# A two-layer graph attention network: the first layer's edge weights and running sums in a PSUM bank, the node chain in one bank instead of two

## The chip, the core and the metric

The kernel runs on one core of one Trainium2 chip. The metric is device time in microseconds of one launch. Most executions of one kernel agree within 0.3%. Five engines matter here: PE (matrix products), DVE (vector work), ACT (activations and copies), POOL (here it issues the indirect DMAs) and SP (here it issues the plain DMAs). PSUM is the small memory that PE writes its products to; it has eight banks of 512 float32 values in each of 128 partitions. SBUF is the large on-chip memory.

## What is computed

A graph of 6250 nodes (16 node types) and 100000 edges (32 edge types), sorted by destination, goes through two layers of typed attention and a residual normalisation. With the names of the reference, cut to what matters:

```
def gt_layer(x, ntype, etype, src, dst, Wk, Wq, Wv, Wa, Watt, Wmsg, pri, skip, g, b):
    k = typed_linear(x, ntype, Wk).reshape(n, H, HS)
    q = typed_linear(x, ntype, Wq).reshape(n, H, HS)
    v = typed_linear(x, ntype, Wv).reshape(n, H, HS)
    kT = jnp.einsum('nhd,htdo->nhto', k, Watt)
    vT = jnp.einsum('nhd,htdo->nhto', v, Wmsg)
    kw = kT[src, :, etype]
    m = vT[src, :, etype]
    a = jnp.einsum('ehd,ehd->eh', kw, q[dst]) * pri[:, etype].T / SQRT_D
    att = edge_softmax(a, dst, n)
    msg = (m * att[:, :, None]).reshape(-1, H * HS)
    hag = jax.ops.segment_sum(msg, dst, num_segments=n)
    h = jax.nn.silu(typed_linear(hag, ntype, Wa))
    alpha = jax.nn.sigmoid(skip[ntype])[:, None]
    h = h * alpha + x * (1.0 - alpha)
    mu = jnp.mean(h, axis=-1, keepdims=True)
    var = jnp.mean((h - mu) ** 2, axis=-1, keepdims=True)
    return (h - mu) * jax.lax.rsqrt(var + 1e-05) * g + b

for l in range(L):
    h = gt_layer(h, ...)
return layernorm(x + h @ ff_w + ff_b)
```

`typed_linear` takes a matrix for each node type; kT and vT hold a row for each node and edge type; L = 2. There are H = 8 heads of HS = 16, so a row of k, q or v has 128 values.

## The kernel before

**Stages.** A first stage sorts the nodes into 49 blocks of 128 (one node to a partition) by type and by number of edges, and builds the first layer's table in DRAM: for each node and edge type one row of 256 values, kT and vT side by side. Then `edges(0)` runs the first layer and, beside it, builds the second layer's table; `edges(1)` runs the second layer and writes the output.

**Gathers.** For a block with K slots (K is the largest number of edges of its nodes), POOL issues K indirect DMAs (L1434). Each brings one table row to each of the 128 partitions. There are 819 in each layer. Behind each stand two small fills of a tile called `pause` (L1440), also on POOL. Four gathers fill one tile `kv` (a chunk, CH = 4); twelve such tiles are in turn, so POOL waits when the oldest is not yet used up.

**A block's edge work, on DVE.** For each chunk: `kv*q` (L1454) and a sum over each head (L1460) give the logits `a`. Then `finished` (L1298 to L1375) does for the block: add the mask, subtract the largest, `Exp` on ACT (L1323), and for each chunk the product of the values with the weights (L1339) and the addition to `acc` (L1346). `acc` has four slots of 128 values, so that a chunk is added in one instruction; at the end a reduction over the four slots gives `sums` (L1367). In the first layer the weights stand in `a` and the sums in `acc`, both in SBUF. In the second layer the query, the weights and the sums stand in a PSUM tile `pair` of the pool `tps` (L1285, L1322, L1334). One block, `TOP`, with 42 slots, has a way of its own in both layers.

**The node chain.** Two to four blocks make a superblock, 15 in all. Thirteen hold nodes of four types; two hold blocks of all 16 types and are called mixed here (`len(types) > TC`). When a superblock's sums are there, the generator `nodes` (L1536) turns the sums (transposes on PE into a tile `hT`), multiplies a copy of `hT` masked by type (`xm`, on DVE, L271) with `wa` for each type, applies the gate, the skip and the normalisation, and turns the result again. In the first layer it then makes k, v and q for the next layer (`wkqv`): k and v are copied from PSUM to SBUF (`kvT0`, `kvT1`, by ACT), q is turned back and stored. From `kvT` PE makes the pieces of the second layer's table (`tb<-bdk,kvT`, L312), ACT copies them to `st` (L320), and POOL scatters each `st` to DRAM (L1672, 98 scatters in all, two for each block). The queries of the first layer, `queries0` (L1219), go through the same steps with `wq0`. All these tiles that are written by PE have the name `nb` and come from the pool `nps`, two banks of PSUM. The pool `tps` has three tiles of two banks. That fills the eight banks.

**The order of the work.** POOL's instructions run in the order of the program. The generators of the node chain and of the queries are advanced by a few steps for each chunk of gathers: `tick` (L1249) spreads a given number of steps (33 for a node chain of the first layer, 42 more when mixed) over the slots of the blocks that follow. A scatter is issued eight such steps after its last piece. On PE, DVE and ACT a scheduler then sets the order; instructions that go through `on` appear in the trace under the line of a helper, L247. The second layer's gathers wait for all 98 scatters.

## Time and profile before

| | us |
|---|---|
| three timed runs | 3146.17, 3147.55, 3155.6 (median 3147.55) |
| the profiled execution's own time | 3152.49 |
| its span, from the first to the last instruction | 3150.6 |
| POOL busy | 2376.3 (75%) |
| DVE busy | 1871.8 (59%) |
| PE busy | 1561.5 (50%) |
| ACT busy | 964.4 (31%) |

The first layer's gathers start at 594 us and its last one at 1887 us of the span; the second layer's start at 1958 us and end at 3105 us. A row that groups instructions reads: line, engine, operation, output and inputs by the program's names, shape, count, then the busy time in us and the mean of one in ns, and behind the bar the time for which the engine was idle just before them, with what ended it. In a row of the timeline the two numbers in front are the start and the duration in us, and in brackets stands how long the engine had been idle before, with what ended that. PE's records hold two passes for each float32 product, so four products are eight records.

### The profile page before, as it was taken

Reading aid. Unit: us, or ns where it says so; the run is one execution under the profiler, and the core shown is the slowest. Engines: PE = TensorE matmul, PEld = TensorE weight load, DVE = VectorE, ACT = ScalarE, POOL = GpSimd, SP = SyncE. Lnnn points to the kernel's source line nnn. Section 1 sums busy time; section 2 is a strip of 40 time slices with the busy share of each in tenths; the row PEclk is TensorE's granted clock in tenths of the full one; section 3 lists DMA queues with packets and bytes.
Section 4 is the critical chain, followed back from the end, with each engine's and each line's share of the span. In section 5 each row is a group of like instructions: output and inputs, shape, how many; then the busy total and the mean of one; then the engine's idle time right before and its main releaser. Section 6 shows DMA issues by size and latency. Waiting matters only on the chain.

```text
span 3150.6 us, 24725 instructions
## 1 busy us (share of the span) xinstructions
PE 1561.5 (50%) x5295; PEld 706.2 (22%) x5295; DVE 1871.8 (59%) x4322; ACT 964.4 (31%) x1599; POOL 2376.3 (75%) x5392
## 2 busy tenths in 40 slices
PE   5999887303675647776688775011221122112112
PEld 2445334101232312332233232000110011001001
DVE  7477655266646656666665553466556675666565
ACT  3887433101444123533354453001100121012111
POOL 3332665588868887888888882888788888888884
PEclk9899766556677767777777686555555556555555
DMA  7999999933777457775688888333333333333331
GB/s 214 421 419 414 390 388 399 299 94 101 256 262 274 157 194 262 279 295 195 233 306 297 304 290 313 104 109 107 99 102 103 110 114 106 100 108 108 98 97 46
DMA packets 174584, 674.80 MB, mean 214 GB/s; under 512 B 52972, under 2 KB 89998, under 8 KB 149374
## 3 DMA queue, kind: packets, MB, share of 16 engines
q0 software_dynamic: 113152, 635.19, 56.1%
q1 hardware_dynamic: 45170, 30.78, 3.4%
q10 hardware_dynamic: 16096, 7.10, 0.9%
q8 instruction: 46, 0.75, 0.1%
q14 instruction: 120, 0.98, 0.1%
HBM read 248.64 MB, written 425.02 MB: 214 GB/s over the span
## 4 chain that ended last, share of the span: by engine, by line
POOL 46%; issue 11%; DMA 10%; DVE 8%; PE 5%; ACT 2%; POOLq 0%; DVEq 0%; ACTq 0%
POOL kv L1434 35%; DMA kv<-tab,ell 9%; POOL pause L1440 7%; PE nb L247 3%; POOL tab L1672 1%; DMA tab<-st,row 1%; DVE kv L1454 1%; POOL out_dram L1704 1%; PE tb L312 1%; DVE kv L247 1%; DVE hs L247 1%; DVE a L1460 1%; DVE acc L247 1%; ACT L247 1%; ACT st L320 1%
## 5 line engine op out<-in xcount | busy, mean ns | idle before, releaser
L1434 POOL DMA_INDIRECT kv<-tab,ell x1638 | 1634.1, 998 | 325.6 <-issue 250.0
L320 ACT COPY st<-tb 128x512 f32<-128x512 f32 (+1 forms) x984 | 677.5, 778 | 555.6 <-PE tb L312 330.4
L1454 DVE TENSOR_TENSOR kv<-kv,tb 128x512 f32<-128x512 f32 (+3 forms) x223 | 143.0, 641 | 449.0 <-DMA kv<-tab,ell 443.6
L1454 DVE TENSOR_TENSOR kv<-kv,q 128x512 f32<-128x512 f32 (+3 forms) x223 | 143.6, 645 | 410.5 <-DMA kv<-tab,ell 404.1
L247 PE MATMUL nb<-ident,hag 128*128 128x128 f32 x98 | 27.1, 417 | 722.2 <-DVE hag L247 722.1
L1440 POOL MEMSET pause<- 128x32 bf16 x3276 | 334.2, 142 | 0.7
L312 PE MATMUL tb<-bdv,kvT 32*128 32x512 f32 x784 | 259.4, 799 | 52.3 <-ACT st L320 51.7
L312 PE MATMUL tb<-bdv,vT 32*128 32x512 f32 x784 | 260.2, 784 | 48.8 <-ACT st L320 45.0
L1460 DVE TENSOR_REDUCE a<-kv 128x32 f32<-128x512 f32 (+2 forms) x446 | 281.5, 634 | 1.2
L1128 POOL DMA_INDIRECT tab<-st,rows x98 | 101.6, 1037 | 199.5 <-ACT st L320 165.3
L247 PE MATMUL nb<-xm,wa 128*128 128x512 f32 (+2 forms) x336 | 187.3, 715 | 106.0 <-DVE xm L247 105.8
L312 PE MATMUL tb<-bdk,kvT 32*128 32x512 f32 x784 | 231.9, 776 | 14.1 <-ACT st L320 13.7
L247 PE MATMUL nb<-xm,wkqv 128*128 128x384 f32 (+2 forms) x504 | 209.5, 579 | 20.8 <-DVE xm L247 20.8
L318 DVE COPY st<-tb 128x512 f32<-128x512 f32 (+1 forms) x192 | 128.7, 708 | 147.6 <-PE tb L312 78.3
L312 PE MATMUL tb<-bdk,kT 32*128 32x512 f32 x784 | 206.0, 783 | 6.5 <-issue 5.8
L247 PEld LDWEIGHTS nb<-ident,hag 128*128 128x128 f32 x98 | 16.1, 205 | 740.5 <-issue 510.5
L247 DVE SCALAR_TENSOR_TENSOR xm<-ntb,nb 128x512 f32<-128x512 bf16 (+2 forms) x304 | 155.3, 562 | 40.0 <-PE nb L247 39.8
L247 PE MATMUL nb<-xm,wq 128*128 128x384 f32 (+2 forms) x168 | 88.5, 678 | 163.4 <-DVE xm L247 163.4
L1672 POOL DMA_INDIRECT tab<-st,row x98 | 104.1, 1062 | 83.7 <-ACT st L320 59.9
L247 PEld LDWEIGHTS nb<-xm,wkqv 128*128 128x128 f32 x504 | 111.7, 228 | 126.0 <-issue 45.5
L247 DVE TENSOR_TENSOR tb<-kv,tb 128x512 f32<-128x512 f32 (+3 forms) x216 | 138.6, 642 | 0.2
L247 PE MATMUL nb<-ident,hs 128*128 128x128 f32 x98 | 33.5, 469 | 205.6 <-DVE hs L247 198.4
(342 smaller groups left out, 2467.8 us busy)
## 6 DMA issues: line engine op xcount, KB each, us to landing
kv<-tab,ell POOLq DMA_INDIRECT x1638
hr<-xrd SPq DMA_DIRECT2D x14, 256.0 KB
hqd<-hs SPq DMA_DIRECT2D x7, 512.0 KB, 3.1
hq<-hqd SPq DMA_DIRECT2D x7, 512.0 KB
xrd<-xr SPq DMA_DIRECT2D x10, 256.0 KB, 23.2
hr<-xrd SPq DMA_DIRECT2D x10, 192.0 KB, 2.8
hqd<-hs SPq DMA_DIRECT2D x5, 384.0 KB
hq<-hqd SPq DMA_DIRECT2D x5, 384.0 KB, 3.2
```

What stands on the lines that cost most here:

```text
L247: put = issue(*args, **kwargs)
L312: stream[nc.tensor] = nc.tensor.matmul(pt[:, b], yT[s, i * P:(i + 1) * P], bd[s, tt, :], start=True, stop=True)
L318: nc.vector.tensor_copy(to, pt)
L320: stream[nc.scalar] = nc.scalar.copy(to, pt)
L1128: put = nc.gpsimd.indirect_dma_start(out=tabs[0].rearrange("(n t) c -> n (t c)", t=16), out_offset=bass.IndirectOffsetOnAxis(ap=rows1[:, t ...
L1434: get = nc.gpsimd.indirect_dma_start(out=kv[:, j - j0, :], out_offset=None, in_=tabs[l][:], in_offset=bass.IndirectOffsetOnAxis(ap=ell[:, ...
L1440: nc.gpsimd.memset(pause[:, at % PAUSES, half], 0.0)
L1454: stream[nc.vector] = nc.vector.tensor_tensor(kk, kk, of.unsqueeze(1).to_broadcast([P, c, D]), op=ALU.mult)
L1460: nc.vector.tensor_reduce(to, kk.rearrange("p k (h d) -> p k h d", h=H), axis=AX.X, op=ALU.add)
L1672: put = nc.gpsimd.indirect_dma_start(out=tabs[1].rearrange("(n t) c -> n (t c)", t=16), out_offset=bass.IndirectOffsetOnAxis(ap=row2[:, tg ...
L1704: put = nc.gpsimd.indirect_dma_start(out=out, out_offset=bass.IndirectOffsetOnAxis(ap=node[:, b:b + 1], axis=0), in_=o[:, i, :], in_offset ...
```

## The change

Three things change together. All are in the arm that the run takes (`fast`).

1. The first layer's weights and running sums go to a PSUM tile `held` of one bank (pool `hold`, one buffer): two slots of sums of 128 values each, and the weights behind them. `Exp` writes the weights there, and the products and additions read and write there. Since the sums are two slots wide and not four, a chunk of four is added in two instructions; the first chunk's first two slots go to the sums as products, and its other two are added afterwards. The block `TOP` keeps its way.
2. For that bank, the pool `nps` of the node chain and the queries has one bank instead of two. A new function `linear_of` takes the output's tile only when the masked copies of `hT` have been made; where a superblock is mixed, `hT` is first copied to SBUF (`h2`), in both layers.
3. A mixed superblock makes k, v and q one after the other, each with masked copies of its own, and no longer k and v from the same copies. The table of steps gives a mixed node chain of the first layer 58 steps more and not 42.

```
+    def linear_of(pool, nps, types, ntb, hT, n, w):
+        types = list(types)
+        if len(types) > TC:
+            h2 = pool.tile([P, SB * P], F32, name="h2", tag="hb")
+            on.scalar.copy(h2[:, :n], hT[:, :n])
+            yield
+            hT = h2
+        some, ps = 2 if len(types) > TC else TC, None
+        for t0 in range(0, len(types), some):
+            xms = list(masked(pool, types[t0:t0 + some], ntb, hT, n))
+            yield
+            if ps is None:
+                ps = nps.tile([P, SB * P], F32, name="nb")
+            for t, xm in xms:
+                on.tensor.matmul(ps[:, :n], w[:, t, :], xm[:, :n],
+                                 start=(t == types[0]), stop=(t == types[-1]))
+            if t != types[-1]:
+                yield
+        return ps
...
-        nps = ctx2.enter_context(tc.tile_pool(name="nps", bufs=2 if fast else 5, space=PSUM))
+        nps = ctx2.enter_context(tc.tile_pool(name="nps", bufs=1 if fast else 5, space=PSUM))
+        hold_ps = ctx2.enter_context(tc.tile_pool(name="hold", bufs=1, space=PSUM)) if fast else None
...
-            ps = nps.tile([P, SB * P], F32, name="nb")
-            yield from linear_steps(npl, types, ntb, hT, k * P, [(ps, wq0)])
+            ps = yield from linear_of(npl, nps, types, ntb, hT, k * P, wq0)
...
-                if l and rest is None:
-                    w = pair[:, 1, D:D + K * H].rearrange("p (k h) -> p k h", h=H)
+                if rest is None:
+                    if l == 0:
+                        held = hold_ps.tile([P, SB * P], F32, name="hold")
+                    w = (pair[:, 1, D:D + K * H] if l else held[:, 2 * D:2 * D + K * H]).rearrange(
+                        "p (k h) -> p k h", h=H)
...
+                    acc = held[:, :2 * D].rearrange("p (k c) -> p k c", k=2)
+                wide = acc.shape[1]
...
+                        parts = [(v, v, j0)] if j else [
+                            (acc, v[:, :wide], j0), (v[:, wide:], v[:, wide:], j0 + wide)]
...
-                        on.vector.tensor_tensor(acc[:, :j1 - j0], kvt[j - 1][:, :j1 - j0, D:],
-                                                acc[:, :j1 - j0], op=ALU.add)
+                        for c0 in range(0 if j > 1 else wide, j1 - j0, wide):
+                            c = min(wide, j1 - j0 - c0)
+                            on.vector.tensor_tensor(acc[:, :c], kvt[j - 1][:, c0:c0 + c, D:],
+                                                    acc[:, :c], op=ALU.add)
...
-                           (42 if l else 33) + (0 if len(sbs[s][2]) == TC else 14 if l else 42),
+                           (42 if l else 33) + (0 if len(sbs[s][2]) == TC else 14 if l else 58),
...
-            y = nps.tile([P, SB * P], F32, name="nb")
-            yield from linear_steps(npl, types, ntb, hT, n, [(y, wa)])
+            y = yield from linear_of(npl, nps, types, ntb, hT, n, wa)
...
-                    for js in ((0, 1), (2,)):
-                        outs += [nps.tile([P, SB * P], F32, name="nb") for _ in js]
+                    for j in range(3):
+                        outs.append(nps.tile([P, SB * P], F32, name="nb"))
```

**Where instructions move.** On PE, at the first superblock's k, v and q (the names: `hs` is the normalised result that is turned, `xm` a masked copy, `wkqv` the three matrices of each type, `tb` a piece of the table, `qT` the query that is turned back), the order before is:

```order
L247 MATMUL nb<-ident,th 128x128 x4
L247 MATMUL nb<-ident,hs 128x128 x4
L247 MATMUL nb<-xm,wkqv 128x512 x12
L312 MATMUL tb<-bdk,kvT_6679 128x512
L247 MATMUL nb<-ident,qT 128x128 x4
```

and now:

```order
L247 MATMUL nb<-ident,th 128x128 x4
L247 MATMUL nb<-ident,hs 128x128 x4
L247 MATMUL nb<-xm,wkqv 128x512 x8
L334 MATMUL tb<-bdk,kvT_6714 128x512
L247 MATMUL nb<-xm,wkqv 128x512 x4
L334 MATMUL tb<-bdk,kvT_6714 128x512
L247 MATMUL nb<-ident,qT 128x128 x4
```

The twelve products are cut: before the last four, which wait for the bank, stands a piece of the table.

On PE, at the first mixed superblock's k, v and q, the order before is:

```order
L247 MATMUL nb<-ident,hs 128x128 x2
L247 MATMUL nb<-xm,wkqv 128x256 x34
L312 MATMUL tb<-bdk,kvT_8476 128x512
L247 MATMUL nb<-xm,wkqv 128x256 x4
L312 MATMUL tb<-bdk,kvT_8476 128x512
L247 MATMUL nb<-xm,wkqv 128x256 x4
```

and now:

```order
L247 MATMUL nb<-ident,hs 128x128 x2
L247 MATMUL nb<-xm,wkqv 128x256 x19
L334 MATMUL tb<-bdk,kvT_8503 128x512
L247 MATMUL nb<-xm,wkqv 128x256
L334 MATMUL tb<-bdk,kvT_8503 128x512
L247 MATMUL nb<-xm,wkqv 128x256
L334 MATMUL tb<-bdk,kvT_8503 128x512
L247 MATMUL nb<-xm,wkqv 128x256
L334 MATMUL tb<-bdk,kvT_8503 128x512
L247 MATMUL nb<-xm,wkqv 128x256 x14
```

Before, k and v run together through all 16 types (32 products) ahead of the first piece; now k's 16 come alone, and the first pieces stand among v's.

On DVE, where the first block's weighted sums are made beside the second block's logits (`kv*q` at L1454 before and L1491 now, the head sums at L1460 and L1497), the order before is:

```order
L247 TENSOR_REDUCE den<-a 128x8
L247 TENSOR_TENSOR acc<-kv,a 128x512
L1454 TENSOR_TENSOR kv<-kv,q 128x4x128
L247 TENSOR_TENSOR kv<-kv,a 128x4x128
L1460 TENSOR_REDUCE a<-kv 128x32
L247 TENSOR_TENSOR kv<-kv,a 128x4x128
L247 TENSOR_TENSOR acc<-kv,acc 128x512
L247 TENSOR_TENSOR kv<-kv,a 128x4x128
L247 TENSOR_TENSOR acc<-kv,acc 128x512
```

and now:

```order
L247 TENSOR_TENSOR hold<-kv,hold 128x256
L1491 TENSOR_TENSOR kv<-kv,q 128x4x128
L247 TENSOR_TENSOR kv<-kv,hold 128x2x128
L247 TENSOR_TENSOR kv<-kv,hold 128x4x128
L1497 TENSOR_REDUCE a<-kv 128x32
L247 TENSOR_TENSOR hold<-kv,hold 128x256
L1491 TENSOR_TENSOR kv<-kv,q 128x4x128
L247 TENSOR_TENSOR kv<-kv,hold 128x4x128
L1497 TENSOR_REDUCE a<-kv 128x32
L247 TENSOR_TENSOR hold<-kv,hold 128x256 x2
```

Products and additions now have one operand named `hold` (PSUM); an addition of 512 values has become two of 256.

35 lines of the change are left out of this document (19 added, 16 removed).

## The prediction

> **What bounds the kernel now.** I read the busy time by stretches first, to see which stage is bound by what. The columns are each engine's busy time and instructions, then the granted clock and the DMA's share and rate.
>
> ```profile
> core 0: us, PE busy (x) PEld busy (x) DVE busy (x) ACT busy (x) POOL busy (x), PEclk, DMA share, GB/s
> 594.00:1887.00 1293.00, 823.45 (x2552) 343.62 (x2554) 786.01 (x1702) 461.60 (x619) 1105.37 (x2542) 0.72 0.67 236
> 1887.00:1960.00 73.00, 42.52 (x160) 19.75 (x156) 27.73 (x56) 30.74 (x44) 13.04 (x17) 0.71 0.86 339
> 1960.00:3105.00 1145.00, 202.74 (x449) 104.44 (x449) 686.13 (x1674) 137.75 (x277) 993.84 (x2497) 0.54 0.35 104
> ```
>
> In both layers POOL is the busiest (1105 of 1293 us, and 994 of 1145). Between the layers lie 73 us in which it has little to do: the second layer's gathers wait for the last scatters. So a change of the first layer counts through three things: how long POOL needs for a gather, how long it waits for others between 594 and 1887, and how long the last node chain takes after that. POOL's groups, of the first layer and then of the second:
>
> ```profile
> L1434 POOL DMA_INDIRECT kv<-tab,ell x821 | 850.2, 1036 | 182.8 <-issue 124.4 <-ACTq L1869 19.4 <-DMA tab<-st,row 13.1
> L1672 POOL DMA_INDIRECT tab<-st,row x98 | 104.1, 1062 | 83.7 <-ACT st L320 59.9 <-issue 18.8 <-DVE st L318 3.9
> ```
>
> ```profile
> L1434 POOL DMA_INDIRECT kv<-tab,ell x787 | 755.3, 960 | 138.1 <-issue 121.0 <-DVE acc L247 7.7 <-DVE hs L247 2.8
> ```
>
> A gather takes 1036 ns in the first layer and 960 ns in the second, and is the same instruction in both. Then POOL's waits in the first layer (total, times, longest):
>
> ```profile
> POOL kv L1434 <- issue: 124.4, 745, 0.3
> POOL tab L1672 <- ACT st L320: 59.9, 10, 22.7
> POOL kv L1434 <- DVE acc L247: 12.9, 8, 11.6
> ```
>
> The 124.4 us are some 0.16 us behind each instruction and stay. The waits for ACT are scatters that stand ready on POOL before the table piece is made; every gather behind them waits too.
>
> Why gathers are longer in the first layer, the timeline shows:
>
> ```profile
> 1071.49 0.69 DVE L247 TENSOR_TENSOR acc<-kv,acc 128x512 f32<-128x512 f32 x1
> 1071.62 1.38 POOL L1434 DMA_INDIRECT kv<-tab,ell  x1 [0.16 <-issue]
> 1074.66 0.95 POOL L1434 DMA_INDIRECT kv<-tab,ell  x1 [0.15 <-issue]
> 1074.89 0.69 DVE L1454 TENSOR_TENSOR kv<-kv,q 128x512 f32<-128x512 f32 x1
> ```
>
> The gather of 1071.62 starts while an addition with both inputs in SBUF runs (to 1072.18) and takes 0.43 us longer than the one of 1074.66, where such a product starts 0.23 us after the gather. So it is the gather's start that is held, until about the end of the DVE instruction. In the second layer the query, the weights and the sums are read from PSUM, and the excess is nearly gone.
>
> **Gain on POOL.** The excess is (1036 - 960) ns x 821 = 62.4 us; the 98 scatters may add up to the same 76 ns each (7 us) or nothing, I take 4: 66 us in all. How much of it goes? The first layer's DVE groups with two SBUF inputs, and the form that will replace the additions:
>
> ```profile
> L1454 DVE TENSOR_TENSOR kv<-kv,q 128x512 f32<-128x512 f32 x184 | 127.0, 691 | 369.8 <-DMA kv<-tab,ell 364.8 <-issue 4.7
> L247 DVE TENSOR_TENSOR acc<-kv,acc 128x512 f32<-128x512 f32 x135 | 92.3, 684 | 0.0
> L247 DVE TENSOR_TENSOR kv<-kv,a 128x512 f32<-128x512 f32 x135 | 90.9, 683 | 0.0
> L247 DVE TENSOR_TENSOR acc<-kv,a 128x512 f32<-128x512 f32 x49 | 33.4, 682 | 0.0
> L247 DVE SCALAR_TENSOR_TENSOR xm<-ntb,h 128x384 f32<-128x384 bf16 x32 | 16.7, 554 | 3.2 <-PE nb L247 2.7 <-ACT h L247 0.3
> L247 DVE SCALAR_TENSOR_TENSOR xm<-ntb,h 128x256 f32<-128x256 bf16 x32 | 12.1, 415 | 0.0
> L247 DVE TENSOR_TENSOR acc<-kv,acc 128x256 f32<-128x256 f32 x10 | 4.2, 417 | 0.0
> L247 DVE TENSOR_REDUCE sums<-acc 128x128 f32<-128x512 f32 x49 | 50.7, 1034 | 0.0
> ```
>
> The first six sum to 372.4 us. The change takes three of them out (92.3 + 90.9 + 33.4 = 216.6). It leaves `kv*q`, and it adds masked copies from SBUF: each mixed superblock had 32 of them and now has 80 (16 for `wq0`, 16 for `wa`, 48 for k, v and q), so 96 more at (554 + 415)/2 ns = 46.5 us. By share of DVE time 202.3 of 372.4 us stay, and the gain is 66 x 0.46 = 30 us. The other end: `kv*q` mostly starts when its gather lands (364.8 of its 369.8 us of idle time), so it may seldom meet a gather's start. If it never does, the 66 us belong to the other 245.4 us (0.27 each), and the gain is (216.6 - 46.5) x 0.27 = 46 us. I take 36, nearer the first, since the rows don't say how many of the 184 follow without a wait.
>
> On this the Trainium skill's page "SBUF — State Buffer", section "Who interferes with whom", has two rules. One says that a DVE instruction with two SBUF inputs contends with a GpSimd instruction that reads SBUF, held until the end; that agrees with the 1.38 against 0.95 us. The other infers that a `tensor_tensor` does not stall a DMA's descriptor writing, since it takes only the read side; by that the gain would be nothing, and the 1036 against 960 ns speak against it. It is the last rival below.
>
> **Loss in the node chain, between 594 and 1887.** With one bank, three hand-overs are new in each of the 13 plain superblocks. (a) A linear's first product waits until all four masked copies are made and `hT` is given back, not for the first copy alone: three copies more, in the `wa` and in the `wkqv` linear. (b) v's products wait for k's copy, (c) q's for v's. The rows:
>
> ```profile
> L247 DVE SCALAR_TENSOR_TENSOR xm<-ntb,nb 128x512 f32<-128x512 bf16 x84 | 52.5, 681 | 24.1 <-PE nb L247 23.9
> ```
>
> ```profile
> 862.53 12.25 PE L247 MATMUL nb<-xm,wkqv 128*128 128x512 f32 x24
> 862.63 1.01 ACT L320 COPY st<-tb 128x1024 f32<-128x1024 f32 x1 [4.61 <-PE tb L312]
> 867.95 0.59 ACT L247 COPY kvT<-nb 128x512 f32<-128x512 f32 x1 [4.12 <-PE nb L247]
> 874.82 0.59 ACT L247 COPY qT<-nb 128x512 f32<-128x512 f32 x1 [2.85 <-PE nb L247]
> 875.76 0.66 PE L247 MATMUL nb<-ident,qT 128*128 128x128 f32 x4
> 879.71 1.01 POOL L1672 DMA_INDIRECT tab<-st,row  x1 [8.05 <-ACT st L320]
> ```
>
> ```profile
> 1234.47 1.01 POOL L1672 DMA_INDIRECT tab<-st,row  x1 [4.88 <-ACT st L320]
> 1261.91 1.48 POOL L1672 DMA_INDIRECT tab<-st,row  x1 [8.50 <-ACT st L320]
> ```
>
> (a) is 3 x 0.68 = 2.0 us, twice. For (b) and (c) there is a like hand-over in the trace already: from the start of the `qT` copy (874.82) to PE's next product (875.76) pass 0.94 us, so two cost 1.9 us while ACT is free, and up to 1.01 more each where a copy of a table piece is in front. A superblock's chain grows by 4.0 + 1.9 = 5.9 us. What is queued behind it: PE runs in order, so pieces of the table (`tb`) stand behind the waiting products, ACT's `st` copies behind those, then the scatter, and on POOL every gather. Where cover is thick this costs nothing, since PE is idle for 470 of the 1293 us. At least the chains that already make POOL wait pay: the three rows above, 3 x 5.9 = 18 us. At most all 12 ahead of the last pay: 71 us. I take 32, five or six chains, because the burst of 12.25 us that stands before the wait of 8.05 us is the same in every superblock, and because the two mixed ones put PE behind too. On POOL itself five of the 98 scatters now stand six to eight rows later, behind some two more gathers each, and nothing else moves; the gathers in between are issued in either case, so I leave that at nothing. A mixed superblock's extra 16 masked copies for k, v and q (7.8 us of DVE) are spread over the same slots by the 58 steps and lie under DVE's 369.8 us of waiting for gathers; without that cover both would cost 15.5 us.
>
> **DVE's own work.** Additions: the 135 of 684 ns become 270 of 417 (+20 us), and 48 more come for the first chunk (+20 us). The 49 split products cost 2 x 417 instead of 682 ns (+7 us). The reduction over two slots instead of four, 1034 ns now, falls at least to half (-25 us). With the copies above, DVE gains some 70 us of work on 786 in 1293 us. Nothing waits for DVE but the `kv` tiles: the 12.9 us of waits for `acc`. Between 0 and doubling that: I take 6 us.
>
> **Tail and second layer.**
>
> ```profile
> 1917.41 1.42 DVE L247 SCALAR_TENSOR_TENSOR xm<-ntb,nb 128x256 f32<-128x256 bf16 x4 [0.57 <-PE nb L247]
> 1917.89 8.49 PE L247 MATMUL nb<-xm,wkqv 128*128 128x256 f32 x24 [0.52 <-DVE xm L247]
> 1933.10 0.97 POOL L1672 DMA_INDIRECT tab<-st,row  x1 [22.72 <-ACT st L320]
> ```
>
> Here nothing covers the chain. PE now starts at 1917.89; with one bank it starts after the four copies (1918.83), 0.9 us later, and two hand-overs of 0.94 follow: 2.8 us, with the same wait before `wa` 3 to 6 us; I take 4. In the second layer the node chain's `wa` step waits likewise, hidden but for the last superblock (1 us), and 32 masked copies of the mixed superblocks now come from SBUF (15.5 us of DVE at 0.18 to 0.27 of excess each, 3 us): 4 us, between 2 and 6.
>
> **Sum:** -36 + 32 + 6 + 4 + 4 = +10 us. That stands against the profiled execution's 3152.49 us (3162). The median of the three runs is 3147.55, so I forecast 3158 us.
>
> **Rivals.**
> 1. *The slack holds, and the gain decides.* PE idle for a third of the stage speaks for it, and ACT for two thirds. Then only the three waiting chains pay: -36 + 18 + 2 + 4 + 3 = -9 us, and with the higher gain of 46 us -19; some 3133 us. Against it: a POOL that is faster by 36 us comes sooner to the same scatters, so chains that are just in time now become late.
> 2. *The one bank becomes the bound of the first layer.* Each of 12 chains pays its 5.9 us: -36 + 71 + 6 + 5 + 4 = +50, 3197 us. The place is PE's order in front of each scatter; it decides from the point at which PE's added idle time (12 x 5.9) can no longer be placed before a scatter. For it speaks that POOL waits for ACT ten times already; against it that at least nine of the twelve chains don't make it wait today.
> 3. *The gathers don't get shorter*, because something other than DVE's SBUF reads holds them (the scatters' traffic, which the second layer lacks). Then the sum is +46, 3194 us. The pair at 1071.62 and 1074.66 speaks against it.
>
> **How the numbers follow.** Forecast 0.55, first rival 0.22, second 0.18, third 0.05. A change under 0.3% (9.4 us, 3138 to 3157) can't be told from none. My forecast with its own range of 3144 to 3174 gives 0.05 faster, 0.42 same, 0.53 slower; the first rival is nine times in ten faster; the other two are slower. So faster 0.23, same 0.26, slower 0.51. Bounds for 8 in 10: low with the gain of 46 and the smallest losses, -46 + 18 + 0 + 3 + 2 = -23, cut to 3130; high with the lower gain of 30 and the losses at three quarters of their upper ends (0.75 x (71 + 13 + 6 + 6) = 72), +42, 3190.
>
> **What would show it.** The mean of a first-layer gather: 1036 now, some 995 if the gain is 36 us; still 1036 is the third rival. The `kv*q` product should still hold gathers that start inside it. POOL's wait for `st` copies: 59.9 us now, some 95 by my forecast, under 85 by the first rival, over 125 by the second. The stretch from the last gather of the first layer to the first of the second is 71 us now (1887 to 1958); 75 expected. In the second layer a gather should stay near 960 ns. I am wrong in mechanism if POOL's longer waits are for `kv` tiles (DVE) and not for `st`.

## The result, and the profile after

| | before | after |
|---|---|---|
| median of 12 runs each, us | 3153.26 (3146.17 to 3163.51) | 3142.49 (3138.68 to 3150.18) |
| profiled execution: own time, span | 3152.49, 3150.6 | 3141.70, 3139.9 |
| first gather of the first layer | 594.13 | 591.96 |
| its last gather | 1887.02 | 1866.89 |
| first gather of the second layer | 1958.36 | 1942.42 |
| its last gather | 3104.78 | 3092.48 |

The ratio is 0.9965, with a 95% interval of 0.9953 to 0.9977: the change makes the kernel faster by 0.35%, some 11 us. I had forecast 10 us in the other direction; the time itself lies inside my range of 3130 to 3190. By the table's rows the first layer became 18.0 us shorter (1292.9 to 1274.9), the stretch between the layers 4.2 longer (71.3 to 75.5), the second layer 3.6 longer, the end 1.6 longer, and the first layer started 2.2 earlier: -10.8 us, the difference of the spans.

The busy time by the three stretches, in the columns that the prediction explains:

```profile
core 0: us, PE busy (x) PEld busy (x) DVE busy (x) ACT busy (x) POOL busy (x), PEclk, DMA share, GB/s
592.00:1867.00 1275.00, 826.88 (x2530) 336.76 (x2530) 808.17 (x1963) 460.96 (x619) 1065.85 (x2543) 0.74 0.68 239
1867.00:1942.00 75.00, 49.24 (x182) 20.89 (x180) 31.14 (x69) 32.22 (x41) 10.87 (x13) 0.73 0.82 326
1942.00:3093.00 1151.00, 204.95 (x449) 103.65 (x449) 686.30 (x1674) 140.27 (x287) 996.85 (x2500) 0.54 0.35 104
```

In the first layer POOL has 40 us less to do (1105.4 to 1065.9), and only 18 of them came off the stage. DVE has 22 us more (786.0 to 808.2), not the 70 that I had added up. The groups of POOL, first layer and then second:

```profile
L1471 POOL DMA_INDIRECT kv<-tab,ell x819 | 810.7, 990 | 175.6 <-issue 119.8 <-ACTq L1903 20.2 <-DVE acc L247 10.7
L1706 POOL DMA_INDIRECT tab<-st,row x98 | 101.5, 1035 | 105.9 <-ACT st L342 38.4 <-DVE st L340 25.9 <-ACT hold L247 25.2
```

```profile
L1471 POOL DMA_INDIRECT kv<-tab,ell x783 | 752.6, 961 | 139.9 <-issue 121.4 <-DVE acc L247 10.1 <-DVE hs L247 3.1
```

A gather of the first layer fell from 1036 to 990 ns and a scatter from 1062 to 1035; the second layer's stayed (960, now 961). That is 46 x 819 + 27 x 98 ns = 40 us. Ahead of the scatters POOL waits 22 us more than before (83.7 to 105.9). Its waits inside the first layer (592 to 1867) alone:

```profile
POOL tab L1706 <- ACT hold L247: 25.2, 6, 11.3
POOL tab L1706 <- ACT st L342: 16.2, 9, 5.4
POOL kv L1471 <- DVE acc L247: 10.7, 1, 10.7
POOL kv L1471 <- DVE kv L1491: 4.8, 6, 3.4
```

Both upper rows are scatters that wait for ACT; for six of them the profile names the `Exp` that ACT ran beside the copies. Together they are 41.4 us, where the same stretch of before (594 to 1887) has 22.7:

```profile
POOL tab L1672 <- ACT st L320: 22.0, 5, 8.5
POOL tab L1672 <- ACT a L247: 0.7, 3, 0.3
```

So 19 of the 40 us went back there. They did not go back at the scatters that waited before. Counted in their order, the 8th, the 32nd and the 34th of the 98 waited over 1 us then (21.4 us in all, the three scatters that the prediction shows), and now these three go out at once. Eight others ahead of the layer's last gather wait over 1 us in their place (the 1st, 9th, 10th, 29th, 35th, 36th, 40th and 62nd), 39.5 us in all. First the three that waited before, then three of the new ones:

```profile
867.06 1.02 POOL L1706 DMA_INDIRECT tab<-st,row  x1 [0.17 <-issue]
1220.86 1.02 POOL L1706 DMA_INDIRECT tab<-st,row  x1 [0.17 <-issue]
1239.29 1.02 POOL L1706 DMA_INDIRECT tab<-st,row  x1 [0.17 <-issue]
897.88 1.01 POOL L1706 DMA_INDIRECT tab<-st,row  x1 [4.18 <-ACT st L342]
1262.69 1.02 POOL L1706 DMA_INDIRECT tab<-st,row  x1 [11.34 <-ACT hold L247]
1604.93 1.01 POOL L1706 DMA_INDIRECT tab<-st,row  x1 [5.40 <-ACT st L342]
```

One chain of the node work, in the superblock that the prediction showed at 862.53. First the row of before where its masked copies start, then the chain now:

```profile
860.63 2.48 DVE L247 SCALAR_TENSOR_TENSOR xm<-ntb,nb 128x512 f32<-128x512 bf16 x4 [2.66 <-PE nb L247]
```

```profile
862.75 2.48 DVE L247 SCALAR_TENSOR_TENSOR xm<-ntb,nb 128x512 f32<-128x512 bf16 x4 [0.23 <-PE nb L247]
865.38 6.21 PE L247 MATMUL nb<-xm,wkqv 128*128 128x512 f32 x8 [2.66 <-DVE xm L247]
871.62 0.58 ACT L247 COPY kvT<-nb 128x512 f32<-128x512 f32 x1 [9.79 <-PE nb L247]
872.26 3.70 PE L247 MATMUL nb<-xm,wkqv 128*128 128x512 f32 x8 [0.68 <-ACT kvT L247]
876.00 0.59 ACT L247 COPY kvT<-nb 128x512 f32<-128x512 f32 x1 [3.79 <-PE nb L247]
876.94 3.70 PE L247 MATMUL nb<-xm,wkqv 128*128 128x512 f32 x8
880.68 0.58 ACT L247 COPY qT<-nb 128x512 f32<-128x512 f32 x1 [4.09 <-PE nb L247]
887.28 1.02 POOL L1706 DMA_INDIRECT tab<-st,row  x1 [8.35 <-ACT hold L247]
```

The hand-overs are where the diff puts them: PE's products come in three groups, each behind a copy. From the masked copies to the `qT` copy pass 17.93 us (862.75 to 880.68), before 14.19 (860.63 to 874.82). Of the 3.7 us more, 0.7 are the wait for the masked copies (PE starts 2.63 us after the first of them and not 1.90), 1.7 are PE's two pauses behind the copies of k and v, and 1.4 are the products themselves, which take 13.6 us and not 12.25.

### The profile page after: what moved, and what is told of

Its sections match the earlier page's. It is cut to its first block, busy times and chain, and to the rows that moved or that the text cites. A ratio compares the mean times of both kernels' runs of the same rounds, so it can differ in the third digit from the quotient of the medians.

```text
span 3139.9 us, 25059 instructions
## 1 busy us (share of the span) xinstructions
PE 1569.1 (50%) x5295; PEld 698.8 (22%) x5295; DVE 1897.9 (60%) x4596; ACT 967.0 (31%) x1605; POOL 2338.3 (74%) x5392
## 4 chain that ended last, share of the span: by engine, by line
POOL 41%; DVE 11%; issue 10%; DMA 9%; PE 8%; ACT 2%; POOLq 0%; DVEq 0%; ACTq 0%
POOL kv L1471 32%; DMA kv<-tab,ell 8%; POOL pause L1477 7%; PE nb L247 5%; PE tb L334 2%; DVE kv L1491 2%; DVE kv L247 2%; DVE xm L247 2%; DVE hold L247 1%; POOL out_dram L1738 1%; DVE a L1497 1%; DMA tab<-st,row 1%; POOL tab L1706 1%; DVE hs L247 1%; ACT L247 1%
## 5 line engine op out<-in xcount | busy, mean ns | idle before, releaser
L1471 POOL DMA_INDIRECT kv<-tab,ell x1638 | 1597.6, 975 | 332.9 <-issue 246.7
L1491 DVE TENSOR_TENSOR kv<-kv,tb 128x512 f32<-128x512 f32 (+3 forms) x223 | 143.0, 641 | 453.5 <-DMA kv<-tab,ell 445.8
L1491 DVE TENSOR_TENSOR kv<-kv,q 128x512 f32<-128x512 f32 (+3 forms) x223 | 143.6, 645 | 334.2 <-DMA kv<-tab,ell 329.0
L1497 DVE TENSOR_REDUCE a<-kv 128x32 f32<-128x512 f32 (+2 forms) x446 | 281.5, 633 | 1.3
L334 PE MATMUL tb<-bdv,kvT 32*128 32x512 f32 x784 | 247.6, 759 | 44.4 <-ACT st L342 44.0
L247 PE MATMUL nb<-xm,wkqv 128*128 128x384 f32 (+2 forms) x504 | 224.8, 596 | 40.9 <-DVE xm L247 31.2
L1706 POOL DMA_INDIRECT tab<-st,row x98 | 101.5, 1035 | 105.9 <-ACT st L342 38.4
L247 DVE TENSOR_TENSOR hold<-kv,hold 128x256 f32<-128x256 f32 (+1 forms) x410 | 169.2, 413 | 4.8
L247 PE MATMUL nb<-xm,wq 128*128 128x384 f32 (+2 forms) x168 | 81.9, 638 | 142.9 <-DVE xm L247 142.8
L247 DVE SCALAR_TENSOR_TENSOR xm<-ntb,nb 128x512 f32<-128x512 bf16 (+2 forms) x208 | 112.4, 599 | 49.0 <-PE nb L247 49.0
L247 PEld LDWEIGHTS nb<-xm,wa 128*128 128x128 f32 x336 | 87.3, 278 | 245.1 <-issue 166.2
```

The lines of the kernel that those rows point to most:

```text
L247: put = issue(*args, **kwargs)
L334: stream[nc.tensor] = nc.tensor.matmul(pt[:, b], yT[s, i * P:(i + 1) * P], bd[s, tt, :], start=True, stop=True)
L1471: get = nc.gpsimd.indirect_dma_start(out=kv[:, j - j0, :], out_offset=None, in_=tabs[l][:], in_offset=bass.IndirectOffsetOnAxis(ap=ell[:, ...
L1491: stream[nc.vector] = nc.vector.tensor_tensor(kk, kk, of.unsqueeze(1).to_broadcast([P, c, D]), op=ALU.mult)
L1497: nc.vector.tensor_reduce(to, kk.rearrange("p k (h d) -> p k h d", h=H), axis=AX.X, op=ALU.add)
L1706: put = nc.gpsimd.indirect_dma_start(out=tabs[1].rearrange("(n t) c -> n (t c)", t=16), out_offset=bass.IndirectOffsetOnAxis(ap=row2[:, tg ...
```

## The experiments

There were five sets of runs, each with the kernel before beside it, and the chips differ. On one the kernel before takes 3150 to 3154 us, as in the result above; the first two sets and the fourth went to another, where it takes 3375 to 3382 us. Each ratio is to the kernel before in the same set. Groups 1 and 2 below are from the faster chip (but for e14), and groups 3 and 4 from the slower one.

**1. The change taken apart.** Four kernels in one set, beside the kernel before at 3154.07 us: the change once more (c2_change); the kernel before with two-slot sums alone, sums and weights in one SBUF tile (e8_two_slots_alone); the change with the held tile in SBUF (e9_sbuf_third); the shared bank alone (e10_bank_third).

```
e8: before, with the change's code for the sums, and
+  held = ep.tile([P, CH, D], F32, name="acc", bufs=1).rearrange("p k c -> p (k c)")
e9: the change, with
-  held = hold_ps.tile([P, SB * P], F32, name="hold")
+  held = ep.tile([P, CH, D], F32, name="acc", bufs=1).rearrange("p k c -> p (k c)")
e10: the change without the pool hold; weights in a, sums four slots wide in acc (SBUF)
```

> The changed kernel once more, as the control of this call. Theory (POOL's chain of gathers sets the end where no engine waits for its instructions, so that the gain of some 41 us reaches the end; where the engines wait for instructions, as in the two calls before, the node chain sets it and only the loss shows): if the kernel before takes about 3150 us here, the ratio is 0.995 to 0.998; if it takes about 3375 us, it is 1.015 to 1.02. Rival (the sign turned by the runs that happened to be taken): the ratio doesn't go with the time of the kernel before.

> The kernel before with the sums two slots wide alone, sums and weights in one SBUF tile, node chain and queries on two banks as before: 242 more DVE instructions and nothing else. Theory (DVE has room): within 0.3% of the kernel before, first-layer gather mean at 1036 to 1056 ns, DVE's wait for gathers shorter by about the added busy time. Rival (DVE's additions add to the chain): slower by 0.3 to 0.9%, the second being the difference between the two earlier pairs of runs with the held tile in SBUF and with one bank alone.

> The change with the held tile in SBUF (third time). Theory: if the kernel before takes about 3150 us, the loss without the gain: mean first-layer gather 1035 to 1056 ns and the time 20 to 45 us above the change's; if it takes about 3375 us, within 0.5% of the change's. Rival (the gather gain is hidden on either chip): within 0.3% of the change's time in both cases.

> One shared bank alone (third time): weights and four-slot sums in SBUF as before. Theory: 20 to 32 us over the kernel before in either case, gather mean 1035 to 1056 ns. Rival (the bank costs only where instructions are late): under 10 us over the kernel before if that takes about 3150 us.

| | us | ratio, 95% interval | gather, ns | scatter, ns | wait ahead of scatters, us |
|---|---|---|---|---|---|
| two slots alone (e8) | 3153.16 | 0.9994 [0.9983, 1.0006] | 1031 | 1065 | 88.5 |
| one bank alone (e10) | 3181.12 | 1.0091 [1.0073, 1.0108] | 1051 | 1127 | 87.6 |
| both, held tile in SBUF (e9) | 3177.64 | 1.0080 [1.0066, 1.0094] | 1051 | 1084 | 94.5 |
| the change (c2) | 3142.61 | 0.9959 [0.9945, 0.9973] | 994 | 1028 | 103.3 |

So PSUM for the held tile is worth 35.0 us (e9 to c2), the shared bank costs 27.1, and the two-slot sums cost nothing on this chip (0.9 us less alone, 3.5 less beside the shared bank). The theory holds for c2 and e9, and for e10, which falls within the 20 to 32 us. For e8 it holds in time (the ratio's interval includes 1), while its gathers, 1031 ns, stay just under the 1036 to 1056 expected.

What I had not expected stands in e10's rows of POOL, first layer:

```profile
L1465 POOL DMA_INDIRECT kv<-tab,ell x819 | 860.8, 1051 | 169.5 <-issue 126.0 <-ACTq L1897 19.4 <-DVE acc L247 11.3
L1700 POOL DMA_INDIRECT tab<-st,row x98 | 110.5, 1127 | 87.6 <-ACT st L342 27.1 <-DVE st L340 25.7 <-ACT a L247 17.9
```

```profile
L1471 POOL DMA_INDIRECT kv<-tab,ell x819 | 814.3, 994 | 174.8 <-issue 118.1 <-ACTq L1903 20.3 <-DVE acc L247 10.4
L1706 POOL DMA_INDIRECT tab<-st,row x98 | 100.7, 1028 | 103.3 <-ACT st L342 37.7 <-DVE st L340 25.5 <-ACT hold L247 24.0
```

The first pair is e10, the second c2. Alone, the bank hardly makes POOL wait: 87.6 us ahead of the scatters against 83.7 before. Its cost up to the second layer (21.7 us: 1385.9 from first gather to first gather, before 1364.2) is in the instructions themselves: gathers (1051 - 1036) x 819 = 12.3 us, scatters (1127 - 1062) x 98 = 6.4, and those 3.9 of waits. From e10 to c2 gathers and scatters shorten by 57 x 819 + 99 x 98 ns = 56 us, and POOL's waits lengthen by 15.7 + 5.3 = 21: 35 us are left. A shorter gather brings POOL to the same scatter sooner, and part of the gain is spent there: the five scatters that wait over 1 us ahead of the last gather in e10 all wait longer in c2 (the 9th of the 98, for one, 6.24 us in e10 and 8.21 in c2).

An extreme case shows how a bank can lengthen gathers (e10, POOL and DVE, in one mixed superblock):

```profile
1420.37 6.87 POOL L1465 DMA_INDIRECT kv<-tab,ell  x1 [0.15 <-issue]
1420.51 1.02 DVE L247 SCALAR_TENSOR_TENSOR xm<-ntb,h 128x384 f32<-128x384 bf16 x2
1421.44 0.69 DVE L247 TENSOR_TENSOR kv<-kv,a 128x512 f32<-128x512 f32 x1
1422.05 0.69 DVE L247 TENSOR_TENSOR acc<-kv,acc 128x512 f32<-128x512 f32 x1
1422.65 1.02 DVE L247 SCALAR_TENSOR_TENSOR xm<-ntb,h 128x384 f32<-128x384 bf16 x2
1423.58 0.69 DVE L1485 TENSOR_TENSOR kv<-kv,q 128x512 f32<-128x512 f32 x1
1424.19 0.69 DVE L247 TENSOR_TENSOR kv<-kv,a 128x512 f32<-128x512 f32 x1
1424.79 0.69 DVE L247 TENSOR_TENSOR acc<-kv,acc 128x512 f32<-128x512 f32 x1
1425.39 1.02 DVE L247 SCALAR_TENSOR_TENSOR xm<-ntb,h 128x384 f32<-128x384 bf16 x2
1426.33 0.68 DVE L1491 TENSOR_REDUCE a<-kv 128x32 f32<-128x512 f32 x1
1427.24 0.20 POOL L1471 MEMSET pause<- 128x32 bf16 x2
```

One gather takes 6.87 us: it is held through a whole row of DVE instructions with two SBUF inputs that follow each other without a gap, and ends some 0.9 us after the last of them gives way to a reduction with one input. The masked copies `xm<-ntb,h` of a mixed superblock, which read a copy of `hT` in SBUF in this kernel, join products and additions into such a row.

This is not the rule, as a count over all 819 gathers of the first layer shows. They are sorted by whether a DVE instruction runs when the gather starts that has two inputs in SBUF (by the tiles that it names):

| | it runs: gathers, mean ns | it doesn't: gathers, mean ns |
|---|---|---|
| before | 252, 1217 | 567, 955 |
| one bank alone (e10) | 275, 1240 | 544, 955 |
| both, held tile in SBUF (e9) | 291, 1219 | 528, 959 |
| the change (c2) | 155, 1157 | 664, 956 |

So the excess is where the prediction looked for it. In c2, 93 gathers start inside an addition to `hold` and 77 inside a product with it, which have one PSUM input each; they take 964 and 956 ns on average. Most held gathers wait for one instruction alone: 246 of the 275 in e10 end at most 0.9 us after the one that runs at their start, also where another of the kind follows at once. The other 29 are held longer, and they are what the bank adds: their excess over 955 ns is 24.3 us in all, where before has 13.2 us in 25 such gathers, while the excess of those held for one instruction is nearly the same (54.1 and 52.8 us). Why these few are held for more than one instruction, the records don't show.

**2. The masked copies out of SBUF; v beside the bank.** e15 is the change with that copy of `hT` in a tile of the table's pool (PSUM), in the first layer; e16 gives v's products of the plain superblocks such a tile besides. e14 is the same kernel as e15 on the slower chip.

```
e15: -  h2 = pool.tile([P, SB * P], F32, name="h2", tag="hb")
     +  h2 = tps.tile([P, 2, SB * P], F32, name="tb")[:, 0]
e16, besides, for v (j == 1):
     -  ps = nps.tile([P, SB * P], F32, name="nb")
     +  ps = tps.tile([P, 2, SB * P], F32, name="tb")[:, 0]
```

> The change with the copy of h of the mixed superblocks (first layer) in a table tile, PSUM, instead of SBUF: the 160 masked copies of the first layer that read two SBUF operands read one. Theory (they hold gathers while both mixed superblocks are worked on): first-layer gather mean 980 to 985 ns against 990 to 994 and the time 3 to 9 us under the change's, that is -14 to -20 us against the kernel before. Rival (the table tile that is held so long delays the pieces, or the copies seldom meet a gather): within 3 us of the change's or slower.

> The copy of h of the mixed superblocks in PSUM, as in e14, once more. Theory (e14 brought the mean first-layer gather to 977 ns against 995 in the same surroundings, 18 ns x 819 = 15 us): where the kernel before takes about 3150 us, 8 to 15 us under the change, that is a ratio of 0.991 to 0.9935 to the kernel before. Rival (what the shorter gathers give is lost to table pieces that wait for the tile): 0.995 or more. Where it takes about 3375 us the ratio stays at 1.015 to 1.02, as in e14.

> The same with v's products of the plain superblocks in a table tile besides (e14 and e4 together). Theory (the waits of v and q for the single bank are a third to a half of the loss in the chains): another 4 to 11 us under e15 where the kernel before takes about 3150 us, and about 0.5% under e15 where it takes about 3375 us. Rival (the table tile that v takes delays the pieces by as much): within 3 us of e15, or slower, where it takes about 3150 us.

Measured beside the kernel before at 3149.98 us: e15 3135.05 (3132.15 to 3139.63), ratio 0.9952 [0.9938, 0.9966]; e16 3139.53, ratio 0.9962 [0.9949, 0.9976]. On the slower chip e14 has 1.0174 [1.0123, 1.0224], and its gathers took 977 ns, a little under the 980 to 985 expected. POOL in e15:

```profile
L1472 POOL DMA_INDIRECT kv<-tab,ell x819 | 801.6, 979 | 175.6 <-issue 119.7 <-ACTq L1904 19.3 <-DVE acc L247 10.9
L1707 POOL DMA_INDIRECT tab<-st,row x98 | 100.3, 1023 | 107.3 <-ACT st L343 35.8 <-ACT hold L247 30.5 <-DVE st L341 25.5
```

Against c2 the gathers are 12.7 us shorter in all (814.3 to 801.6), so the copies did hold them; 4.8 us of it go back in waits (103.3 to 107.3, 174.8 to 175.6), and the first layer is 6.5 us shorter (1275.2 to 1268.7). By medians e15 is 7.6 us under c2, by ratios 0.07%, and the ratios' intervals overlap: less than the 8 to 15 us expected, and by its ratio the rival's case (0.995 or more). Its median is the lowest of all kernels that were run, but a gain over the change is not shown. e16 is no faster than e15, so the rival's time came there: POOL's waits for ACT inside the layer are 51.7 us in e16 (40.4 and 11.3) and 47.0 in e15, so v's bank of its own did not shorten them.

**3. Weights or sums.** The weights stay in the bank, the two-slot sums go to SBUF. It ran on the slower chip, so only the gathers speak.

```
e13: -  acc = held[:, :2 * D].rearrange("p (k c) -> p k c", k=2)
     +  acc = ep.tile([P, CH, D], F32, name="acc", bufs=1)[:, :2]
```

> The change with the weights alone in the PSUM bank; the two-slot sums stand in SBUF. So the products v*w have one PSUM operand, and the additions have both operands in SBUF again. Theory (a gather or scatter is held while DVE instructions with two SBUF inputs follow one another without a gap; each kind that is left prolongs the stretches): the sums carry more than half of the gain, first-layer gather mean 1015 to 1030 ns against 990 (change) and 1051 (all in SBUF), time +8 to +18 us against the kernel before. Rival (the gain goes by share of DVE time of each kind: products 120, additions 165 us): gather mean 1026 ns and +9 us; rival 2 (breaking the stretches at the products is enough): gather mean under 1005 ns and the time within 5 us of the change's.

The mean gather was 1014 ns, where both in SBUF had 1042 (e5) and both in PSUM 995 (c1) on that chip. So 28 of 47 ns go with the weights, that is with the products `kv*w`, though they are the smaller part of DVE's time (118 of 281 us in c2). Two profiles of the same kernel differ by up to 7 ns here (988 and 995, e4 and e12), so that the weights carry at least half is likely and not sure. The theory (sums more than half, 1015 to 1030 ns) misses its range by a nanosecond, and both rivals (1026, and under 1005) miss. That a product with a PSUM input breaks the rows of DVE instructions fits the count: of the 23 us by which e13's gathers are shorter than e5's, 15 are in the gathers that are held for more than one instruction (39.9 us beyond 955 ns each in e5, 24.7 in e13). The products write to SBUF as before, and gathers inside them are no longer held (956 ns above), so one input in PSUM is enough there. The additions write to PSUM too, and no run parts their input from their output. The time, 1.0163 [1.0105, 1.0221], doesn't tell e13 from the change there.

**4. The slower chip.** Ten more runs went there, most with edits that stand above already. e1 and e5 are e9; e2 and e6 are e10; c1 is the change; e4 and e12 give v a table tile (as in e16, in the change); e3 and e11 give the node chain its second bank back and the table two tiles; e7 is the kernel before with the second layer's query read from SBUF.

```
e3, e11: nps bufs=1 -> 2; tps bufs=3 -> 2
e7: -  nc.scalar.copy(pair[:, 1, :D], got[s][0][:, i, :])
    -  return pair[:, 1, :D], pair
    +  return got[s][0][:, i, :], pair
```

> The changed kernel with the tile of weights and sums in SBUF instead of PSUM; still two slots wide, still one bank for the node chain. Theory (where the tile lies is what shortens the gathers; the bank, the chain and DVE's extra instructions only cost): the mean first-layer gather goes from 989 ns back to about 1035 or, with the mixed superblocks' copies from SBUF, 1045; some 40 us slower than the changed kernel, about 30 us slower than the kernel before (ratio 1.009). Rival (the gathers are shorter because of the other timing of the work, as by the narrower additions or the cut node chain): the gathers stay near 990 ns and the time within 10 us of the changed kernel (ratio 0.997 to 1.000).

> Parts 2 and 3 of the change alone: one bank for node chain and queries, the first layer's weights and four-slot sums in SBUF as before. Theory: gathers as in the kernel before, 1036 to 1045 ns; POOL's waits between the layer's first and last gather some 20 us longer than before, the stretch between the layers 4 us longer, the second layer 4 us: ratio about 1.010. Rival A (the longer waits of the changed kernel come from a faster POOL that runs into the same chain, not from the bank): these waits stay as before, ratio about 1.002. Rival B (DVE's extra instructions cost, not the bank): ratio about 1.000 here and clearly less than in the run with the tile in SBUF.

> The changed kernel with two banks for the node chain again, paid for by two tiles of two banks instead of three for the table pieces (and the second layer's queries). Theory: the chain's waits (mid-layer +21 us, tail +4 us against before) shrink, unless the pieces lack their third tile; if the pieces have room, ratio about 0.989 to before. Rival (the third tile is needed, since pieces of the table are what scatters wait for): POOL waits longer for ACT than in the changed kernel, ratio 1.00 or more; the second layer slows as well, since a block's query, weights and sums take a tile there.

> The changed kernel with v's products of a plain superblock in a tile of the table pieces' pool, so that they wait for no bank of the node chain and q's products wait only for k's copy. Theory (hand-overs between k, v and q cost about a third of the added wait): POOL's mid-layer waits fall by 5 to 10 us and the stretch between the layers by 2 us; ratio to before about 0.994. Rival (the wait for all four masked copies, or the mixed superblocks, make the added waits): within 3 us of the changed kernel, ratio 0.9965.

> The changed kernel itself, as the control for the runs beside it, since the last four ran on a chip where the kernel before took 3375 us and not 3153. If the chip is like the first, ratio 0.9965 to before. If instructions reach the engines later there (POOL, ACT and DVE waited on their instruction supply in the last four runs), the longer chain costs more: ratio above 1.

> The changed kernel with weights and sums in SBUF, once more beside the control. Theory (the tile's place is worth some 41 us of POOL's time): gathers near 1045 ns against 990, and 35 to 45 us slower than the control on the same chip (by ratio, 0.011 to 0.014 more). Rival (POOL only waits longer when its gathers are shorter, so the place is worth less): under 20 us slower than the control.

> The one bank alone (weights and four-slot sums in SBUF), once more beside the control. Theory: gathers near 1050 ns; 25 to 35 us slower than the kernel before on a chip like the first (ratio 1.008 to 1.011), of which 10 to 20 us are longer gathers by the mixed superblocks' copies from SBUF and the rest POOL's waits. Rival (DVE's narrower additions make the added waits): ratio under 1.004 here, and over 0.005 less than in the run with the two-slot tile in SBUF.

> The kernel before, with the second layer's query read from SBUF and not copied to PSUM (one ACT copy a block less); the product kv*q is then the only two-input SBUF product of that layer. Theory (a gather that starts inside such a product is held): the second layer's mean gather rises from 960 ns to 970 to 985, 10 to 20 us in all, ratio 1.003 to 1.006; the first layer's gathers stay at 1036. Rival (the scatters' traffic in the first layer makes its gathers longer): the second layer's gathers stay at 960, ratio 1.000.

> The change with two shared banks again, paid for with two tiles for the table's pieces (and the second layer's queries) instead of three. The change stands at -11 us against the kernel before where that takes about 3150 us. Theory (the shared bank costs some 20 us inside the first layer, by handing over one by one): if two table tiles cost nothing, -25 to -35 us against the kernel before. Rival (the three table tiles are what keeps ACT's copies ahead of the scatters): slower than the change by 5 us or more, with POOL's wait for the copies to st up. If the kernel before takes about 3375 us, nothing is told apart (1.010 to 1.018).

> The change with v's products of the plain superblocks in one of the table's tiles, so that v needn't wait for k's copy. Theory (the waits of v and q for the bank are a third to a half of the loss in the chains): -15 to -22 us against the kernel before. Rival (the table tile that v takes delays the pieces by as much): -11 us or worse, POOL's wait for st up. If the kernel before takes about 3375 us, nothing is told apart.

| | ratio, 95% interval | gather of the first layer, ns |
|---|---|---|
| c1, the change | 1.0181 [1.0145, 1.0217] | 995 |
| e1, e5, held tile in SBUF | 1.0136 [1.0106, 1.0166], 1.0169 [1.0141, 1.0197] | 1045, 1042 |
| e2, e6, one bank alone | 1.0106 [1.0071, 1.0140], 1.0083 [1.0054, 1.0113] | 1056, 1052 |
| e3, e11, two banks, two table tiles | 1.0138 [1.0110, 1.0167], 1.0123 [1.0056, 1.0190] | 999, 998 |
| e4, e12, v in a table tile | 1.0136 [1.0105, 1.0166], 1.0120 [1.0079, 1.0160] | 988, 995 |
| e7, query from SBUF | 0.9987 [0.9958, 1.0016] | 1049 |

Here the change is slower than before by 1.8%, as c1's expectation allowed for on such a chip, though its gathers shorten as on the other chip. c1 and e5 differ by the place of the held tile alone, and have the same time within their intervals, so e5's theory (35 to 45 us between them) falls. POOL's scatters in c1, then in e5:

```profile
L1706 POOL DMA_INDIRECT tab<-st,row x98 | 100.5, 1026 | 278.7 <-ACT st L342 179.7 <-ACT hold L247 48.6 <-DVE st L340 26.5
```

```profile
L1705 POOL DMA_INDIRECT tab<-st,row x98 | 105.9, 1081 | 205.4 <-ACT st L342 119.3 <-ACT acc L247 38.5 <-DVE st L340 23.3
```

The gathers give 47 x 819 ns = 38 us, and the waits ahead of the scatters take 73 in these two executions (by the medians of all runs c1 is 8 us longer than e5, by the profiled ones 36). On this chip 40 of c1's 98 scatters wait over 1 us for ACT or DVE, where c2 has 15, and 33 do so in e7, whose first layer is that of the kernel before. So the node chain already sets much of POOL's pace there, and a shorter gather mostly turns into a longer wait.

The single bank alone costs as much as on the other chip (1.0106 and 1.0083, there 1.0091). What is new is a price for the two-slot sums: e5 is e6 with them (and with the weights in their tile), in the same set, and the intervals of the two don't overlap (1.0169 and 1.0083); in the first set e1 and e2 differ by the same edit and by less (1.0136 and 1.0106, intervals that overlap). So the change's 1.8% is the bank's 0.8 to 1.1, the sums' 0.3 to 0.9, and no gain from PSUM to set against them. Why sums that cost nothing on the faster chip (e8) cost something here was not tested.

The runs that return a bank in one way or another (e3, e11, e4, e12) lie some 0.5% under c1 by the middle of the ratios. But they come from other sets, their intervals overlap with c1's, and e1, which returns none, lies with e3 and e4 of its own set (1.0136, 1.0138 and 1.0136), so no gain is shown. Of the forecasts for the time, those of e2 (1.010) and e6 (1.008 to 1.011) came; those of e1, e3 and e4 were worked out for the faster chip and fall here.

Where this chip loses time against the other is in the waits of ACT, here between 592 and 1860 us, of c1 and then of c2:

```profile
ACT st L342 <- remote: 117.1, 25, 15.2
ACT st L342 <- issue: 64.8, 21, 9.0
ACT kvT L247 <- issue: 39.5, 5, 13.0
```

```profile
ACT st L342 <- issue: 17.1, 8, 4.2
```

"remote" is a release from another core or an unknown queue, and "issue" is time in which the profile shows nothing that was waited for. In the same program on the faster chip no engine has a "remote" wait at all. On the slower one DVE and POOL have some too, and so has e7 (`ACT st L320 <- remote` 161 us from 590 to 2155). So these pauses tell why the chip is slower with either kernel, and not by themselves why the change's sign turns. The expectations of c1 and c2 call them waits for instructions; no run shows that. What they are stays open.

e7 asked whether the query's place holds the second layer's gathers: they took 966 ns against 959 in the profile of before, less than the 970 to 985 of the theory and more than the rival's 960, and the time did not change. 24 of its gathers start inside a `kv*q` and take 1167 ns on average. In the first layer it is 58 of them in before (1251 ns), some 17 of the 68 us by which all gathers together exceed 0.95 us each; 55 such gathers are left in c2, and in e15 `kv*q` is most of the excess that remains (14 of 22 us).

## Why the forecast was wrong, step by step

| step of the sum | forecast, us | measured, us |
|---|---|---|
| shorter gathers and scatters | -36 | -40 in the rows |
| node chain between 594 and 1887 | +32 | +19 (POOL's waits for ACT, 22.7 to 41.4) |
| DVE's own work | +6 | nothing by the sums alone (e8); all other idle time of POOL in the layer grew by 3 (187.6 to 209.2 in all, less the 19) |
| stretch between the layers | +4 | +4.2 |
| second layer | +4 | +3.6, and 1.6 at the end |

With the 2.2 us by which the first layer starts earlier, the measured column gives -11.

**What held.** The gain's mechanism and size: gathers are held by DVE instructions with two SBUF inputs, and moving one input to PSUM frees them, since c2 and e9 differ in nothing but the place of the tile (994 and 1051 ns), and the count above finds the excess at just those starts. The prediction left `kv*q` in and let the new masked copies hold gathers, and both do (e15). The Trainium skill, page "SBUF — State Buffer", section "Who interferes with whom", infers that a `tensor_tensor` doesn't stall a DMA's descriptor writing. I read this as a case against the gain; the gain came, but the page is not refuted by it. A gather also reads its row numbers (`ell`) from SBUF, which falls under that section's other rule, and no run here parts the reading from the writing of descriptors. The stretch between the layers came out as forecast. So did the size of the second layer's term, of which the gathers' rows (960 and 961 ns) show about 1 us and not 3. A chain's growth at k, v and q was forecast as 3.9 us and measured as 3.7, in part by luck: the wait for the copies was 0.7 us and not 2.0, and 1.4 us of slower products were not in the sum.

**What failed** is the price of the node chain: "I take 32, five or six chains". The step assumed that a chain's 5.9 us reach POOL in full wherever a chain is late, with the three scatters that waited before as the least (18 us). The measured 19 lies next to that 18 by luck, since those three scatters don't wait any more and others do. What the runs show is that the longer chain by itself costs POOL hardly any waiting: with the bank alone (e10) it waits 3.9 us more ahead of all scatters, and there too the three that waited before go at once. (Its gathers and scatters are 18.7 us longer, which gives the chains some time, so 3.9 is the least that the chain costs.) The longer waits come with the shorter gathers: from e10 to c2 gathers and scatters shorten by 56 us and 21 come back. I had named this ("a POOL that is faster by 36 us comes sooner to the same scatters") and added it as a further loss of chains, where it is a share of the gain. The bank's own cost of 27 us is mostly in those longer gathers and scatters, of which the sum had a part only, under the gain. That the new order of PE, with pieces of the table between k, v and q, is what freed the three scatters is a guess that no run tested.

The second mis-sized term is DVE's +6. I had added 46.5 us for the copies from SBUF without taking off those from PSUM that they replace; DVE's work grew by 22 and not by 70 us. 32 and 6 instead of 19 and 3 are 16 us, the 40 instead of 36 us that the gathers gave are 4, and the other rows and the earlier start about cancel: this is the way from +10 to -11.

The first rival, "the slack holds, and the gain decides", with its -9 us and a chance of 0.22, gave nearly the measured time. Its condition, that the slack holds, is borne out by e10; its price, "only the three waiting chains pay", is not, so its 18 us were luck as well. Its signpost was POOL's wait for `st` under 85 us; the waits for ACT and DVE ahead of scatters, together 89.5 (38.4 + 25.9 + 25.2), lie between its bound and my 95. The second rival fell on this chip. On the slower one the loss is about as large as the rival's, but the bank alone makes up only about half of it, and nothing in the profile of before tells how the same program runs elsewhere. The third fell with the 990 ns.

## What to carry to other kernels

Where an engine issues transfers and waits for a chain beside it, a shorter transfer and a later chain can't be added as two terms: ask for each wait how much of the gain it will take back, and don't price a later chain by the places that wait now, since a new order of work moves the waits. When a buffer is taken from one use, look at what that use reads instead: here the masked copies from SBUF, 160 in the first layer where before has 64, cost 12.7 us in held gathers (c2 to e15). Measure a change of under 1% that trades one engine's time for another's slack on more than one chip before it is believed.

## What the hardware showed that was not expected

- A gather is held only if a DVE instruction with two SBUF inputs runs when it starts: 252 of 819 in before, 1217 ns on average, against 955 ns for the others, none of which takes over 1.0 us. With one of the two inputs in PSUM it isn't held (964 and 956 ns in c2).
- A held gather mostly ends 0.8 us after that one instruction, though others of the kind follow at once. About one in ten is held for longer, up to 6.87 us in e10; why is open.
- The same program took 3142.61 us on one chip and 3437.17 on another, and the change's sign turned with it (0.9959 and 1.0181). The granted clock of the two profiled executions was close (0.675 and 0.659); pauses of several engines for which the profile shows no cause inside the core appear on the slower chip alone, with either kernel.
